# Making the gated layer's node tables inside the attention layer's loop

## The chip, the cores and the metric

The kernel runs on one core of a Trainium2 chip. The metric is device time in microseconds (us) of one execution. Five engines work side by side and meet only through semaphores: TensorE (PE in the profile; its weight loads are listed apart as PEld), VectorE (DVE), ScalarE (ACT), GpSimd (POOL) and SyncE (SP), which here only issues transfers. Each engine executes its own list of instructions in order: an instruction that waits holds up everything behind it on that engine, and nothing on the others unless they wait for it. Transfers between device memory and on-chip memory are issued by an engine's queue (SPq, ACTq) and run beside the engines.

## The reference

Four graph layers run one after the other on 3125 nodes of 128 numbers, with 50,000 edges that come sorted by destination. After each layer its result is added to the input and every row is normalized (mean taken off, divided by the standard deviation). Cut to what matters:

```python
x = ln(x + L0(x))   # 3 x relu(A_norm @ (x @ W) + b), A_norm: weighted adjacency, normalized
x = ln(x + L1(x))   # attention, 4 heads of 32:
                    #   e = sum(leaky_relu(h_l[dst] + h_r[src]) * att);  softmax over a node's edges
                    #   out[dst] += h_r[src] * alpha
x = ln(x + L2(x))   # gated:  z = concat(x[dst], x[src], edge_attr)
                    #   x + segment_sum(sigmoid(z @ W_f + b_f) * softplus(z @ W_s + b_s), dst)
x = ln(x + L3(x))   # 10 x gelu(ln(A_norm @ (x @ W) + b)), plus gelu(ln(x @ res_W + res_b))
```

In the gated layer `z @ W` splits in three: a product of the destination's row, one of the source's row, one of the edge's attributes. The first two need to be worked out once per node, not once per edge. They are the layer's two node tables: `to_dst` (row of a node times the first third of both weight matrices, plus the bias, kept as three bf16 parts that add up to the f32 value) and `to_src` (row times the second third, f32).

## The kernel before

Nodes are cut into 25 row tiles of 128 (`NT`), edges into 392 chunks of 128 (`NCH`), and the chunks into 28 stretches of 14 (`NS`, `SC`). A stretch is worked on in four blocks of 4, 4, 3 and 3 chunks. Because the edges are sorted by destination, a stretch touches one window of 128 consecutive nodes, whose first node is looked up at run time; neighbouring windows overlap, and a stretch's partial sums are handed to the next by a shift matrix.

The stages follow one another. **L0** builds the normalized adjacency matrix into device memory (a "bank" of 35 pieces, about 1.15 MB each) while its first convolution runs, then runs convolutions two and three as dense products with that matrix (`Convolutions`, L620-697; a few pieces stay resident on chip as `adj_k`, the others are streamed as `adj`). In the second half of L0 the attention layer's edge data are prepared too (`Attention.prepare`, L1057). **L1**, the attention layer, is `l1_sorted` (L1149-1341). **L2**, the gated layer, is `l2_sorted` (L1344-1568). **L3** (L1571-1637) runs ten dense convolutions with the same bank.

The loops of L1 and L2 are written out as software pipelines: several stretches are in flight, each in another step. The order on each engine is the order in which the program records the instructions. A helper, `InOrder` (L179-192), chains them, so nearly all instructions of the two loops carry line L187 in the profile and are told apart by their tiles.

One iteration `s` of L1's loop (L1303-1340) runs over four blocks `b`:

- `load(s+1)` (b = 0, L1173): SP loads the window's rows (`hl`) and the edges' destinations (`drow`), POOL issues 14 indirect gathers of the sources' rows into `xj` (six buffers).
- `inputs(s, b)` (L1192): PE sums `h_l[dst]` and `h_r[src]` into `zT` (three PSUM buffers): three bf16 products and one f32 product per chunk. ACT and DVE form the leaky relu.
- `logit` (L1210): PE forms the logits `pe`, two blocks behind. `keep_logits` (b = 1) stores them.
- `messages(s-3)` (b = 0, DVE): weights times gathered rows into `msg`. This frees `xj`.
- `add_up(s-3)` (b = 1, PE, L1275): 14 chunks and the shifted sums of the stretch before into `sums`.
- `rows(s-3)` (b = 2) and `finish(s-3)` (b = 3), on DVE and ACT: division, addition of the old row, normalization. The result is the window's new rows, `y`, which SP stores to `after`.

So on PE one iteration is `inputs(s,0)`, `logit`, `inputs(s,1)`, `logit`, `add_up(s-3)`, `inputs(s,2)`, `logit`, `inputs(s,3)`, `logit`. On DVE the end of an iteration is `y` of stretch s-3, and right behind it stand the `messages` of stretch s-2 for the next iteration's `add_up`.

After the loop the whole of `after` is loaded back to `x` (L1341). L2 then begins with a preamble (L1356-1400): it loads and prepares its own edge data (sources, destinations, local indices), writes a copy of `x` to device memory, clears padding rows and loads its weights. Then it makes both tables, a row tile at a time (L1402-1413): PE transposes all tiles of `x`; per tile PE multiplies with the weights (`pp`), DVE adds the bias, ACT and DVE split the sum into three parts (`three_parts`, L1022), SP stores both tables. L2's loop gathers from `to_src` (POOL, `zj`) and cannot start before that table is complete.

Of the kernel before, what the change touches and what calls it, by code (L numbers as in the profile page):

```python
# [10 lines left out]
I32 = mybir.dt.int32  # L11
# [35 lines left out]
def tile_gnn_stack(ctx: ExitStack, tc: tile.TileContext, a: dict, out: bass.AP):  # L47
# [336 lines left out]
    class SortedEdges:  # L384
# [106 lines left out]
        def matrices(self, pool, c0, n):  # L491
# [14 lines left out]
            low = pool.tile([P, CH, P], BF16, name="of_low", bufs=1)[:, :n]  # L506
            ve.tensor_tensor(columns(low), across(self.lows, P // 2), own(self.low, P // 2), op=OP.is_equal)
            heavy = pool.tile([P, 3, CH, P], BF16, name="heavy")[:, :, :n]
# [254 lines left out]
    def l0_sorted(edges, adj, attention):  # L763


        with (
            tc.tile_pool(name="l0", bufs=1) as one,
            tc.tile_pool(name="l0_rows", bufs=3) as rows,
# [18 lines left out]
            with (  # L787
                tc.tile_pool(name="l0_adj", bufs=4) as stream,
                tc.tile_pool(name="l0_hold", bufs=1) as hold,
            ):  # L790
                load_nodes()
                conv.xs[0] = hold.tile([P, NT, D], F32, name="xs0")
                conv.pieces(stream, hold, 6, InOrder(nc.sync))
                attention.prepare(hold, ps, nc.vector)
                for i in (1, 2):
                    conv(conv.xs[i % 2], *layers[i])
                conv.finish()
                conv.end()
# [240 lines left out]


# [108 lines left out]
    def l1_sorted(at):  # L1149
        right, left, before, after, local, logits = at.right, at.left, at.before, at.after, at.local, at.logits  # L1150
        fresh, src_o, dl, att, bias, apart, step = (at.fresh, at.src_o, at.dl, at.att, at.bias, at.apart, at.step)
        with (
# [6 lines left out]
            with (  # L1159
# [7 lines left out]
                pe_, ve, ac, sp = map(InOrder, (nc.tensor, nc.vector, nc.scalar, nc.sync))  # L1167
# [131 lines left out]
                def finish(s):  # L1299
                    sp.dma_start(after[bass.ds(st[s]["first"], P)], normalized(two, st[s], ve))  # L1300
                    st[s] = {"agg": st[s]["agg"]}
# [4 lines left out]
                for s in range(NS + 4):  # L1306
                    for b in range(NK):
                        if b == 0 and s + 1 < NS:
# [32 lines left out]
            nc.sync.dma_start(x, after[:NP].rearrange("(t p) d -> p t d", p=P))  # L1341


    def l2_sorted():  # L1344
# [6 lines left out]
        with (  # L1351
# [4 lines left out]
            to_dst = dram.tile([NP + P, 3, 2 * D], BF16, name="s2_to_dst")  # L1356
            to_src = dram.tile([NP, 2 * D], F32, name="s2_to_src")
            before = dram.tile([NP + P, D], F32, name="s2_before")
            after = dram.tile([NP + P, D], F32, name="s2_after")
            local = dram.tile([NCH * P], BF16, name="s2_local")  # L1360


            src_i = one.tile([P, NCH], I32, name="src_i")
            nc.sync.dma_start(src_i, a["src_c"])
            dst_i = one.tile([P, NCH], I32, name="dst_i")
            nc.sync.dma_start(dst_i, a["dst_c"])
            dl = one.tile([P, NCH], F32, name="dl")
            nc.vector.tensor_tensor(dl.rearrange("p (s c) -> p s c", c=SC),
                                    dst_i.rearrange("p (s c) -> p s c", c=SC),
                                    first_f[:, :NS, None].to_broadcast([P, NS, SC]), op=OP.subtract)  # L1370
            order = one.tile([P, NS, SC], I32, name="order")
            v = a["dst_r"]
            nc.sync.dma_start(order, bass.AP(tensor=v.tensor, offset=v.offset,
                                             ap=[[SC, P], [SE, NS], [1, SC]]))
            lrow = one.tile([P, NS, SC], BF16, name="lrow")
            nc.vector.tensor_tensor(lrow, order, first_f[:, :NS, None].to_broadcast([P, NS, SC]),
                                    op=OP.subtract)
            nc.sync.dma_start(local.rearrange("(s p c) -> p s c", p=P, c=SC), lrow)

            zero = one.tile([P, 3 * D], F32, name="zero")  # L1380
            nc.vector.memset(zero, 0.0)
            zero_b = one.tile([P, 6 * D], BF16, name="zero_b")
            nc.vector.memset(zero_b, 0.0)
            nc.scalar.dma_start(to_dst[NP:].rearrange("p a b -> p (a b)"), zero_b)
            nc.scalar.dma_start(before[NP:], zero[:, :D])
            nc.scalar.dma_start(after[NP - P:NP], zero[:, :D])
            nc.sync.dma_start(before[:NP].rearrange("(t p) d -> p t d", p=P), x)

            w2 = one.tile([D, 3, 2, D], F32, name="w2")
            for s, name in enumerate(("L2_gnn_W_f", "L2_gnn_W_s")):  # L1390
                nc.scalar.dma_start(w2[:, :, s, :], a[name].rearrange("(r k) d -> k r d", k=D))
            b2 = one.tile([P, 2, D], F32, name="b2")
            for s, name in enumerate(("L2_gnn_b_f", "L2_gnn_b_s")):
                v = a[name]
                nc.scalar.dma_start(b2[:, s, :], bass.AP(tensor=v.tensor, offset=v.offset, ap=[[0, P], [1, D]]))
            eps = one.tile([P, 1], F32, name="eps")
            nc.vector.memset(eps, EPS)
            apart = one.tile([P, P], F32, name="apart")
            step = one.tile([P, NS], F32, name="step")
            window_shifts(apart, step, nc.vector)  # L1400

            with tc.tile_pool(name="s2_ps0", bufs=2, space=PSUM) as ps:  # L1402
                xT = transposed_x(one, ps)
                for t in range(NT):
# [296 lines left out]
```

## Time and profile before

| | us |
|---|---|
| time, median of 3 runs (lowest to highest) | 3730.04 (3726.81 to 3734.39) |
| the profiled execution: time / span | 3739.19 / 3736.9 |
| L0: adjacency and first convolution / second and third convolution | 0-361 / 361-672 |
| L1 (attention): start and loop / last `y` | 680-1450 / 1450.1 |
| between L1's last `y` and L2's first gather | 1450.1-1528.5 |
| L2 (gated): loop | 1528.5-2319 |
| L3: ten convolutions | 2319-3737 |

The span is the profiled part of one execution. A line of a timeline gives the start and the duration in us, the engine, the source line, the operation and its tiles as out<-in, how many instructions are merged, and in brackets the idle time before and what ended it ("issue" means that the profile shows nothing that the engine waited for). A line of a group gives count, busy time, the mean of one in ns, and the idle time before such instructions with its releasers. Windows give busy time of each engine, the granted clock of PE as a share of full speed, and the busy share of the DMA engines.

### The profile page before, as it was taken

What the parts mean: (1) busy time and instruction counts of PE and PEld (TensorE: products, weight loads), DVE (VectorE), ACT (ScalarE), POOL (GpSimd) and SP (SyncE); (2) the same over time, 40 slices, a digit from 0 to 9 for tenths busy, and PEclk for the clock granted to TensorE, in tenths of its full rate; (3) what the DMA queues carried; (4) which work ended last, traced back from release to release, by engine and by line L of the source; (5) the groups of instructions that cost most, each with busy time, mean ns of one, the idle gap of its engine ahead of it and who ended that gap; (6) DMA issues with size and microseconds to landing.
All of it is one profiled execution on the core that took longest, in us unless ns stands there. A gap on an engine that the chain in (4) does not pass through costs nothing.

```text
span 3736.9 us, 35807 instructions
## 1 busy us (share of the span) xinstructions
PE 2962.6 (79%) x12881; PEld 1905.5 (51%) x12909; DVE 1632.0 (44%) x4381; ACT 886.0 (24%) x1404; POOL 817.4 (22%) x863
## 2 busy tenths in 40 slices
PE   2898999346667575366666666999999999999998
PEld 2665455235666563155555554555555555555554
DVE  5995112124545455265656656522222222222234
ACT  0332001100111112254544445211111111111112
POOL 3210000544555530445454451000000000000000
PEclk8999999667667677678787888999999999999999
DMA  1345977222323224444444443867667667666665
GB/s 51 131 148 183 337 250 248 76 58 66 74 73 80 66 68 96 148 120 140 121 141 122 132 134 111 283 213 232 217 210 226 213 219 235 208 210 230 220 209 187
DMA packets 420199, 605.98 MB, mean 162 GB/s; under 512 B 76655, under 2 KB 386748, under 8 KB 419996
## 3 DMA queue, kind: packets, MB, share of 16 engines
q1 hardware_dynamic: 373176, 516.45, 43.2%
q0 software_dynamic: 32320, 79.09, 7.6%
q10 hardware_dynamic: 14516, 8.07, 0.7%
q8 instruction: 103, 1.69, 0.2%
q14 instruction: 84, 0.69, 0.1%
HBM read 541.08 MB, written 62.61 MB: 162 GB/s over the span
## 4 chain that ended last, share of the span: by engine, by line
PE 70%; issue 13%; DVE 9%; DMA 3%; POOL 2%; another core or an unknown queue 2%; ACT 1%; SPq 0%; POOLq 0%; DVEq 0%; ACTq 0%
PE acc L674 41%; PE sums L187 7%; PE pz L187 7%; PE zT L187 5%; PE acc L187 3%; PE pe L187 2%; POOL xj L215 2%; PE side L187 2%; PE po L689 2%; DVE heavy L187 2%; DVE z L187 1%; DVE of_low L187 1%; DVE of_pair L187 1%; DMA x<-s_after 1%
## 5 line engine op out<-in xcount | busy, mean ns | idle before, releaser
L674 PE MATMUL acc<-adj_k,xs 128*128 128x460 f32 (+1 forms) x3180 | 1213.1, 537 | 1.3 <-DMA adj_k<-bank 1.3
L674 PEld LDWEIGHTS acc<-adj_k,xs 128*128 128x128 f32 x3180 | 598.9, 190 | 558.2 <-issue 501.3
L215 POOL DMA_INDIRECT xj<-s_right,src_o x392 | 372.0, 949 | 655.2 <-ACT parts L1142 338.5
L215 POOL DMA_INDIRECT zj<-s_to_src,src_i x392 | 370.7, 946 | 527.6 <-DVE z L187 256.8
L187 PE MATMUL sums<-msg,of_edge 128*128 128x132 f32 (+1 forms) x1568 | 290.3, 337 | 210.8 <-issue 194.4
L674 PE MATMUL acc<-adj,xs 128*128 128x460 f32 (+1 forms) x1020 | 404.2, 543 | 2.1 <-DMA adj<-bank 2.1
L187 PEld LDWEIGHTS sums<-msg,of_edge 128*128 128x128 f32 x1568 | 259.9, 244 | 233.1 <-issue 216.6
L187 PE MATMUL pz<-w,eaT 128*128 128x256 f32 x784 | 266.5, 425 | 83.0 <-issue 43.5
L704 DVE SCALAR_TENSOR_TENSOR v<-po,dinv,three 128x128 f32<-128x128 f32 x250 | 71.1, 344 | 576.0 <-PE po L689 574.8
L674 PEld LDWEIGHTS acc<-adj,xs 128*128 128x128 f32 x1020 | 192.8, 191 | 186.3 <-issue 174.4
L187 DVE TENSOR_TENSOR z<-pz,zj 128x1024 f32<-128x1024 f32 (+1 forms) x112 | 121.9, 1088 | 309.4 <-remote 241.2
L187 PE MATMUL zT<-ident,xj 128*128 128x128 f32 x784 | 156.7, 330 | 121.5 <-issue 111.0
L187 PEld LDWEIGHTS zT<-ident,xj 128*128 128x128 f32 x784 | 140.5, 238 | 155.8 <-issue 139.5
L187 PE MATMUL pz<-td,of_node 128*128 128x256 bf16 x1176 | 208.2, 289 | 13.7 <-DVE of_node L187 8.4
L187 ACT ACTIVATE leaky<-zT 128x512 f32<-128x512 f32 (+1 forms) x112 | 60.3, 541 | 625.2 <-PE zT L187 362.4
L187 DVE TENSOR_TENSOR leaky<-zT,leaky 128x512 f32<-128x512 f32 (+1 forms) x112 | 68.9, 616 | 316.6 <-ACT leaky L187 193.2
L716 ACT ACTIVATE rs<-rs 128x4 f32<-128x4 f32 (+1 forms) x91 | 18.6, 205 | 786.0 <-DVE rs L715 786.0
L187 ACT ACTIVATE soft<-z 128x1024 f32<-128x1024 f32 (+1 forms) x112 | 106.4, 950 | 388.2 <-DVE z L187 245.5
L187 PE MATMUL pe<-att,leaky 128*128 128x4 f32 x784 | 117.0, 262 | 102.1 <-issue 95.8
L187 PEld LDWEIGHTS pz<-w,eaT 128*128 128x128 f32 x784 | 133.0, 213 | 105.9 <-issue 52.6
L187 PEld LDWEIGHTS pe<-att,leaky 128*128 128x128 f32 x784 | 125.1, 231 | 102.1 <-issue 94.4
L187 PEld LDWEIGHTS <-of_node 128*128 128x128 bf16 x1176 | 123.0, 105 | 90.5 <-issue 21.7
(195 smaller groups left out, 3309.8 us busy)
## 6 DMA issues: line engine op xcount, KB each, us to landing
adj_k<-bank SPq DMA_DIRECT2D x268, 1150.0 KB
adj_k<-bank SPq DMA_DIRECT2D x50, 912.5 KB
bank<-strip SPq DMA_DIRECT2D x6, 5750.0 KB
adj<-bank SPq DMA_DIRECT2D x14, 1150.0 KB
eaT<-in_ea_t SPq DMA_DIRECT2D x56, 256.0 KB
drow<-s_local SPq DMA_DIRECT2D x28, 448.0 KB
eaT<-in_ea_t SPq DMA_DIRECT2D x56, 192.0 KB
drow<-s_local SPq DMA_DIRECT2D x56, 128.0 KB
```

The source lines that it names most:

```text
L187: ins = getattr(self.engine, name)(*args, **kwargs)
L215: after_writers(nc.gpsimd.indirect_dma_start(out=to, out_offset=None, in_=table[:NP, :], in_offset=bass.IndirectOffsetOnAxis(ap=index[:, c ...
L674: lanes.tensor.matmul(acc[:, :c1 - c0], xs[:, t, :], k[:, q, :c1 - c0], start=(t == 0), stop=(t == NT - 1))
L689: lanes.tensor.matmul(po[:, t - t0, :], self.aggT[:, t * P:(t + 1) * P], w, start=True, stop=True)
L704: lanes.vector.scalar_tensor_tensor(to[:, t - t0, :], sums[:, t - t0, :], dinv[:, t:t + 1], bias, op0=OP.mult, op1=OP.add)
L716: nc.scalar.activation(rs[:, :n], rs[:, :n], AF.Sqrt)
```

## The change

The two tables are made in L1's loop, from `y` of each stretch, while it is on chip. `next_rows(s, stage)` does it in five stages, each placed at the head of a block: at b = 0 of the iteration after `y` PE transposes `y` and ACT copies the result (stage 0), at b = 1 PE multiplies with the weights, ACT evicts the source half and SP stores it (1), then DVE adds the bias and ACT makes the first part (2), and DVE and ACT make the second (3) and third (4), which SP stores at the head of the next iteration. The transpose and the product use the loop's `zT` buffers. The loop is one iteration longer. There are 28 windows in place of 25 tiles; rows in two windows are written twice.

A class `Gated` loads and prepares the layer's edge data and weights in the second half of L0, beside those of the attention layer. L2's preamble, the copy of `x`, the reload of `x` behind L1 and the table loop are gone: L2 reads L1's `after` as its old rows, and one set of in-order chains serves L1 and L2.

The longer-lived tiles take room from others: 5 adjacency pieces stay resident in L0 in place of 6, and 8 in L3 in place of 9; `l0_rows` has two buffers in place of three; the one-buffer tile `of_low` becomes a part of `heavy`, whose third part is made in place.

```diff
-            low = pool.tile([P, CH, P], BF16, name="of_low", bufs=1)[:, :n]
+            heavy = pool.tile([P, 3, CH, P], BF16, name="heavy")[:, :, :n]
+            low = heavy[:, 2]
...
-            tc.tile_pool(name="l0_rows", bufs=3) as rows,
+            tc.tile_pool(name="l0_rows", bufs=2) as rows,
...
-                conv.pieces(stream, hold, 6, InOrder(nc.sync))
+                conv.pieces(stream, hold, 5, InOrder(nc.sync))
                 attention.prepare(hold, ps, nc.vector)
+                gated.prepare(hold, nc.vector, attention.dl)
...
+        def prepare(self, scratch, ve, dl):
...
+            zero = scratch.tile([P, 2 * D], F32, name="zero_g")
+            ve.memset(zero, 0.0)
+            nc.sync.dma_start(self.to_src[NP - P:NP], zero)
+            nc.sync.dma_start(self.after[NP - P:NP], zero[:, :D])
+            nc.sync.dma_start(self.src_i, a["src_c"])
+            dst_i = scratch.tile([P, NCH], I32, name="dst_g")
+            nc.sync.dma_start(dst_i, a["dst_c"])
+            ve.tensor_tensor(self.dl.rearrange("p (s c) -> p s c", c=SC), dst_i.rearrange("p (s c) -> p s c", c=SC),
+                             first_f[:, :NS, None].to_broadcast([P, NS, SC]), op=OP.subtract)
+            lrow = scratch.tile([P, NCH], BF16, name="lrow_g")
+            ve.tensor_copy(lrow, dl)
+            nc.sync.dma_start(self.local.rearrange("(s p c) -> p s c", p=P, c=SC),
+                              lrow.rearrange("p (s c) -> p s c", c=SC))
...
                 def finish(s):
-                    sp.dma_start(after[bass.ds(st[s]["first"], P)], normalized(two, st[s], ve))
-                    st[s] = {"agg": st[s]["agg"]}
+                    t = st[s]
+                    y = normalized(two, t, ve)
+                    sp.dma_start(after[bass.ds(t["first"], P)], y)
+                    st[s] = {"agg": t["agg"], "first": t["first"], "y": y}
+
+                def next_rows(s, stage):
+
+                    t = st[s]
+                    if stage == 0:
+                        yT = ps_z.tile([D, 4 * P], F32, name="zT")[:, :P]
+                        pe_.transpose(yT, t.pop("y"), ident)
+                        t["yT"] = two.tile([D, P], F32, name="yT", bufs=1)
+                        ac.activation(t["yT"], yT, AF.Copy)
+                    if stage == 1:
+                        t["pp"] = pp = ps_z.tile([P, 4 * P], F32, name="zT")
+                        pe_.matmul(pp, t.pop("yT"), gated.w2[:, :2].rearrange("k r s d -> k (r s d)"),
+                                   start=True, stop=True)
+                        t["parts"] = two.tile([P, 3, 2 * D], BF16, name="parts", bufs=1)
+                        t["row"] = two.tile([P, 2, 2 * D], F32, name="row", bufs=1)
+                        ac.activation(t["row"][:, 1], pp[:, 2 * D:], AF.Copy)
+                        sp.dma_start(gated.to_src[bass.ds(t["first"], P)], t["row"][:, 1])
+                    if stage == 2:
+                        ve.tensor_add(t["row"][:, 0], t.pop("pp")[:, :2 * D],
+                                      gated.b2.rearrange("p s d -> p (s d)"))
+                    if stage > 2:
+                        ve.tensor_sub(t["row"][:, 0], t["row"][:, 0], t["parts"][:, stage - 3])
+                    if stage > 1:
+                        ac.activation(t["parts"][:, stage - 2], t["row"][:, 0], AF.Copy)
+                    if stage == 4:
+                        sp.dma_start(gated.to_dst[bass.ds(t["first"], P)], t["parts"])
+                        st[s] = {"agg": t["agg"]}
...
-                for s in range(NS + 4):
+                for s in range(NS + 5):
                     for b in range(NK):
+                        for r, stage in ((s - 5, b + 4), (s - 4, b)):
+                            if 0 <= r < NS and stage < 5:
+                                next_rows(r, stage)
...
-            nc.sync.dma_start(x, after[:NP].rearrange("(t p) d -> p t d", p=P))
...
-            nc.sync.dma_start(before[:NP].rearrange("(t p) d -> p t d", p=P), x)
...
-                xT = transposed_x(one, ps)
-                for t in range(NT):
-                    pp = ps.tile([P, 2, 2, D], F32, name="pp")
-                    nc.tensor.matmul(pp, xT[:, t * P:(t + 1) * P], w2[:, :2], start=True, stop=True)
-                    h = two.tile([P, 2, 2, D], F32, name="h")
-                    nc.vector.tensor_add(h[:, 0], pp[:, 0], b2)
-                    nc.scalar.activation(h[:, 1], pp[:, 1], AF.Copy)
-                    parts = two.tile([P, 3, 2, D], BF16, name="parts")
-                    evict = three_parts(parts, h[:, 0])
-                    nc.sync.dma_start(to_src[t * P:(t + 1) * P, :].rearrange("p (s d) -> p s d", d=D), h[:, 1])
-                    nc.sync.dma_start(to_dst[t * P:(t + 1) * P].rearrange("p i (s d) -> p i s d", d=D), parts)
...
-            conv.pieces(stream, one, 9)
+            conv.pieces(stream, one, 8)
```

## The prediction

> **What bounds the kernel now.** I read the slices of the page first, then windows for each stage, then the timelines of the two places that the change touches. The windows:
>
> ```profile
> core 0: us, PE busy (x) PEld busy (x) DVE busy (x) ACT busy (x) POOL busy (x), PEclk, DMA share, GB/s
> 820.00:1400.00 580.00, 382.36 (x2296) 342.74 (x2318) 294.29 (x988) 62.78 (x165) 292.45 (x308) 0.71 0.29 72
> 1450.00:1530.00 80.00, 38.49 (x75) 13.54 (x75) 35.75 (x89) 37.78 (x101) 1.23 (x2) 0.71 0.63 161
> 2352.00:3736.00 1384.00, 1368.12 (x4010) 721.59 (x4008) 433.81 (x1565) 272.98 (x348) 0.00 (x0) 1.00 0.67 219
> ```
>
> L3 is PE's: 1368 of 1384 us busy at the full clock. L1's steady loop (820-1400) fills no engine: PE 66% at a granted clock of 0.71, DVE 51%, POOL 50%, ACT 11%. Its period is 25 us a stretch (`add_up` starts on PE at 998.8, 1024.0, 1048.8, 1073.8). A loop with no full engine is bound by a chain that goes round between them. The table stage (1450-1530) has nothing beside it but itself. Its edges:
>
> ```profile
> 1450.11 0.34 DVE L187 TENSOR_SCALAR y<-u,mv,rs 128x128 f32<-128x128 f32 x1
> 1451.52 2.43 SPq L187 DMA_DIRECT2D s_after<-y  x1
> 1457.24 0.80 SPq L1341 DMA_DIRECT2D x<-s_after  x1
> 1465.84 3.84 PE L603 MATMUL xT_ps<-ident,x 128*128 128x128 f32 x16 [19.48 <-DMA x<-s_after]
> 1528.46 0.95 POOL L215 DMA_INDIRECT zj<-s_to_src,src_i  x1 [159.31 <-ACT parts L1025]
> ```
>
> From the last `y` to L2's first gather: 1528.46 - 1450.11 = 78.4 us, of it 15.7 for a store and a reload, the rest for 25 transposes and tiles.
>
> The loop, where the change puts this work, on PE in one stretch, and DVE's `y` (three answers of the timeline):
>
> ```profile
> 1006.17 0.38 PE L187 MATMUL zT<-of_node,hl 128*128 128x512 bf16 x1
> 1007.84 0.38 PE L187 MATMUL zT<-of_node,hl 128*128 128x512 bf16 x1 [1.29 <-issue]
> ...
> 1017.04 0.37 PE L187 MATMUL zT<-ident,xj 128*128 128x128 f32 x1 [1.75 <-issue]
> 1018.45 0.57 PE L187 MATMUL zT<-ident,xj 128*128 128x128 f32 x1 [1.04 <-issue]
> 1018.81 1.28 PE L187 MATMUL pe<-att,leaky 128*128 128x4 f32 x6
> 1019.95 1.44 PE L187 MATMUL zT<-of_node,hl 128*128 128x512 bf16 x3
> 1021.19 1.91 PE L187 MATMUL zT<-ident,xj 128*128 128x128 f32 x8
> 1022.89 1.28 PE L187 MATMUL pe<-att,leaky 128*128 128x4 f32 x6
> 1024.03 1.23 PE L187 MATMUL sums<-msg,of_edge 128*128 128x132 f32 x4
> ```
> ```profile
> 1014.16 0.35 DVE L187 TENSOR_SCALAR y<-u,mv,rs 128x128 f32<-128x128 f32 x1
> ```
> ```profile
> 1022.86 0.94 POOL L215 DMA_INDIRECT xj<-s_right,src_o  x1 [7.15 <-PE zT L187]
> ```
>
> PE starts `inputs(s,0)` at 1006.17, 8.3 us before the `y` of the stretch four back is there (1014.51). It then crawls, an instruction in 1.4 to 2.1 us for no reason but "issue", until shortly after POOL's run of 14 gathers (998.5-1015.7). Then it goes densely but at half speed: the second block takes 3.1 us here, 1.7 in a dense stretch at 872.3. `add_up` follows at 1024.0. POOL has been idle 7 us by then, so gathers are not what is late.
>
> **The change part by part** (against the profiled execution, 3739.2 us, which lies 9.2 above the median).
>
> *D, the gap between L1 and L2, goes.* Left after the last `y`: transpose (0.5), eviction (0.35), product (the pair of passes 1.0 to 1.9), eviction (0.4), a store. The pair store-reload above needed 5.7 us from issue to the follower's issue. That is 0.5+0.35+1.6+0.4+5 = about 8. Gain 78.4 - 8 = **-71**. `to_dst` follows some 2 us behind `to_src`; its reader, PE's `pz`, first ran 9 us after the first gather, so that is covered.
>
> *B, the loop.* Per stretch PE gets one transpose (rows of L603: 272 to 475 ns) and one product of 128x512 (L1406, two passes of 592 to 1222 ns, mean 787), ACT five evictions of about 0.4, DVE three of 0.42, SP two stores. By busy time alone that is 2 us of PE. The place matters more: the transpose is PE's first instruction of the iteration and waits for `y`. Behind it stand `inputs(s,0)`, `logit`, the product, `inputs(s,1)`, `logit` and `add_up`, so all that PE did ahead of `y` now comes after it. I took each steady and draining stretch (23 of them, the `y` of stretches 1 to 23), and put after `y` the whole sequence, once at the dense rows (transpose 0.27 + 1.70 + 0.73 + product 1.02 + 1.70 + 0.73 = 6.15 us) and once at half-speed rows (0.47 + 3.15 + 1.28 + 1.90 + 3.15 + 1.28 = 11.2), and compared with where `add_up` starts today. In the stretch shown: 1014.5+6.15 = 1020.7, 3.4 us before 1024.0 (hidden), or 1025.7, 1.7 after it. With `y` at 1194.4 and `add_up` at 1197.2 it is +3.3 or +8.4; with 1087.0 and 1099.3, -6.2 or -1.1. Counting only positive ones, the 23 sum to +32 at dense and +103 at half speed. With every stretch counted, a gain too where PE would be earlier, they sum to -22 and +94. PE will have stood idle for 148/23 = 6.4 us before each `y`, and half-speed rows are what follows such pauses, but it will also have spared instructions for which it crawls now; I take the middle of the positive sums, +68. DVE's and ACT's extra instructions stand in the same round (`y`, `messages`, `rows`): two of the eight, 0.42 each, 0.8 x 23 = +19; none if idle time takes them, which DVE has (286 of 580 us). **B = +87**, bounds -22 and +103+19 = +122; all 148 us of lead lost, and 2 us of new work in each, would be 148+46 = +194.
>
> A rule weighed here. The Trainium skill, "TensorE: Matmul & The Clock Gate", section "HAM oscillation — how this bites in real kernels", says that pauses of PE beyond about 3.4 us put its clock back to half, each time anew. By the rule every one of the 20 stretches whose lead is above 3.4 us would pay half speed, and the sum is near +103. The rows bear it out after the crawl (3.1 against 1.7 us above) but show the clock back before the end of `add_up`, which loses only its first half.
>
> *The drain of L1* (the last four stretches, `y` 11 to 13 us apart): `add_up` starts 0.75 us behind `y` today and then waits for `messages`. Transpose, eviction and product come before it: about 0.5+0.5+1.9 = 2.9, less 0.3 that overlaps: 4 x 2.6 = **+10** (0 to +12).
>
> *A, L0's second half.* SP's queue today has the load of `order`, then the first `adj` (issued 369.29, landed 377.14; PE waits). The new order puts before it two clearing stores, `wide`, `dst_g`, and the store of `lrow_g`, which waits for `dl`, made from `order` (373.07). Such a store of 28-byte runs took 3.62 us to issue (at 1458.15). The first `adj` is issued at about 373.6+3.6 = 377 in place of 369: **+8** (+4 to +12). ACT's `s_local` stores, PE's `side` and the rest of `prepare` are unchanged. The other new loads (`src_i`, weights, biases) stand earlier in SP's list, beside the first convolution, while PE computes: 0.
>
> *C, L1's start.* With no preamble behind it, three of L3's resident pieces (3 x 1150 KB) are now loaded at L1's start, beside the first gathers and `hl`. DMA's share there is 0.19, and the pieces are 11 to 12 us of transfer at the 300 GB/s that the heaviest stretches move (317 from 361 to 400): **+4** (0 to +10).
>
> *E, L3's start.* Today two of those pieces enclose the last store, and the load of `x` behind them is issued 9.1 us after the store (2319.22, 2328.32), against 5.7 in the unloaded case at 1451.52; it takes 10.4 to land against 8.5. Without them **-6** (-9 to -3).
>
> *At nothing:* one piece less resident: L3 loads 27 in place of 26 per layer (DMA share 0.67 to 0.70) and L0's two layers 30 in place of 29 (0.69 to 0.84), under a PE that is full; if that cover went, 1.15 MB at 300 GB/s, 3.8 us a layer. `heavy` in place and `l0_rows` at two: their DVE runs beside a full PE; `of_low` had one buffer anyway, so bounds are -2 and +4. The reload of `x` behind L1 and the ACT table load are in D.
>
> Sum: -71 + 87 + 10 + 8 + 4 - 6 = **+32**. 3739.2 + 32 = 3771; less 9.2 for the median, **3762 us**.
>
> **Rivals.**
> 1. *The loop swallows it (faster).* The crawl ends near the arrival of `y` (1018 against 1014.5 above), and an instruction not issued in it is not lost if PE is fed while it waits. Then PE starts after `y` with a full supply and B is between -22 and +32. For it: six of the 23 stretches come out earlier even at half speed. Against it: 11 come out later even at dense speed. It decides below B = 55, where the sum is zero. With B = +5 the sum is -50: 3680.
> 2. *The wait adds in full (much slower).* If PE's round through `y` becomes the bound, with the pause, half clock and crawl all in it, B goes to +194 or so: sum +139, 3869. For it: `messages` stand right behind `y` and free `xj` for POOL, so a late `y` moves the next gathers and their crawl as well. Against it: in 12 of the 23 stretches `add_up` comes 6 to 14 us after `y` today, so there is room.
> 3. *The gap remains in part.* L2's first gathers wait for something else (the last `to_dst`, `td`, instruction supply: today the first `z` is made at 1555, 27 us behind the first gather), and D is -45: sum +58, 3788. For it: L2's PE crawls during its first gathers today; but those gathers start 70 us sooner either way.
>
> **How the numbers follow.** My forecast (B between +47 and +150) has 0.55, rival 1 0.30, rival 2 0.05, rival 3 0.10. Of the forecast's 0.55 some 0.04 lie within 0.2% (7.5 us, about what a measurement of this kernel can tell from no change), of rival 1's 0.30 some 0.03. So faster 0.27, same 0.07, slower 0.66. The forecast's own range is 3722 to 3825. For 8 in 10 the range reaches down into rival 1 to B = +10 (3685) and up past rival 3 to 3835.
>
> **What would show it.** In the profile after: `y` to L2's first `zj` about 8 us (D; over 25 makes rival 3); on PE a wait of the transpose for `y` at the head of each iteration, around 6 us; spacing of `add_up` about 28 to 29 us where it is 25 (25 or less makes rival 1, over 33 rival 2); DVE's spacing of the last four `y` 14 to 15; the first `adj` issued at 376 or later; L3's load of `x` some 6 us behind the store. The prediction is wrong if PE's crawl shortens by as much as the wait is long, or grows with the longer period.

## The result and the profile after

The changed kernel takes 3793.26 us (median, 3785.81 to 3797.35) beside 3731.53 for the kernel before: ratio 1.0164 (95% interval 1.0144 to 1.0184), 62 us slower. The forecast was 32 us slower. The direction and the range hold the result; the forecast's size is about half of what came.

Chips differ here, and no number below can be understood without this: with unchanged code the kernel before takes 3700 to 3740 us on some chips and 3207 us on others. The first measurement and two later sets of runs met the first kind, four sets the second. On the first kind PE crawls in the two loops: beside POOL's runs of gathers it issues an instruction only now and then, for no reason that the profile shows (the prediction shows such a stretch). I call the two kinds chips with and without the slow stretch. Each kernel is compared only with the kernel before on its own chip.

The stages in the traces, each worked out from start or end times of the named instructions (us):

| | before | after | | before, second chip | after, second chip |
|---|---|---|---|---|---|
| first product of the second convolution | 377.1 | 393.1 | | 376.6 | 392.0 |
| from there to L1's first gather | 303.3 | 302.7 | | 303.3 | 302.8 |
| first gather to `y` of stretch 1 | 191.5 | 190.3 | | 182.7 | 191.7 |
| `y` of stretch 1 to 21 (per stretch) | 491.1 (24.55) | 590.7 (29.53) | | 497.3 (24.87) | 585.6 (29.28) |
| `y` of 21 to 27 | 87.5 | 91.1 | | 81.0 | 91.4 |
| last `y` to L2's first gather | 78.0 | 8.9 | | 78.8 | 8.9 |
| L2's gathers to its last `y` | 790.7 | 790.7 | | 789.6 | 790.7 |
| last `y` to the end | 1417.7 | 1416.0 | | 1418.6 | 1417.2 |
| span | 3736.9 | 3783.6 | | 3727.9 | 3780.2 |

The steady loop's window (same columns as in the prediction):

```profile
850.00:1450.00 600.00, 359.56 (x1993) 304.79 (x2014) 269.39 (x903) 91.24 (x241) 269.00 (x283) 0.70 0.28 72
```

Only ACT is fuller (15% for 11%); PE is at 60% where it was 66%, DVE and POOL at 45% where they were at 51% and 50%. The loop waits more; no engine has become its bound. One stretch of the loop, from `y` to the next `y`, on PE, on DVE and on POOL (timelines of the changed kernel):

```profile
1093.17 0.45 PE L187 MATMUL zT<-ident,y 128*128 128x128 f32 x1 [3.40 <-DVE y L187]
...
1094.69 1.91 PE L187 MATMUL zT<-ident,xj 128*128 128x128 f32 x8
1096.40 1.28 PE L187 MATMUL pe<-att,leaky 128*128 128x4 f32 x6
1097.54 2.05 PE L187 MATMUL zT<-w,yT 128*128 128x512 f32 x2
...
1102.01 0.73 PE L187 MATMUL pe<-att,leaky 128*128 128x4 f32 x6
1102.60 3.40 PE L187 MATMUL sums<-msg,of_edge 128*128 128x132 f32 x28
1105.83 0.39 PE L187 MATMUL sums<-agg,shift 128*128 128x132 f32 x2
...
1111.92 0.17 PE L187 MATMUL pe<-att,leaky 128*128 128x4 f32 x1 [1.03 <-issue]
1112.64 0.56 PE L187 MATMUL pe<-att,leaky 128*128 128x4 f32 x2 [0.56 <-issue]
1114.74 0.48 PE L187 MATMUL zT<-of_node,hl 128*128 128x384 bf16 x1 [1.53 <-issue]
1115.45 0.81 PE L187 MATMUL zT<-of_node,hl 128*128 128x384 bf16 x2 [0.23 <-issue]
1116.87 1.44 PE L187 MATMUL zT<-ident,xj 128*128 128x128 f32 x6 [0.60 <-issue]
```
```profile
1106.23 0.41 DVE L187 TENSOR_TENSOR row<-zT,b 128x256 f32<-128x256 f32 x1
1117.00 0.29 DVE L187 COPY agg<-sums 128x132 f32<-128x132 f32 x1 [10.36 <-PE zT L187]
...
1122.51 0.34 DVE L187 TENSOR_SCALAR y<-u,mv,rs 128x128 f32<-128x128 f32 x1
```
```profile
1096.92 0.95 POOL L215 DMA_INDIRECT xj<-s_right,src_o  x1 [12.62 <-PE zT L187]
```

The transpose waits 3.40 us for `y`, as foreseen. But the costly wait is another: `add_up` ends at 1106.2, and DVE takes its sums only at 1117.00, 10.8 us later, when PE's crawl is over. In the stretch of the kernel before that the prediction shows, the crawl lay in `inputs(s,0)`, beside DVE's work on `y`, and `agg` came 1.9 us after `add_up`'s end:

```profile
1002.01 0.39 PE L187 MATMUL sums<-agg,shift 128*128 128x132 f32 x2
1004.29 0.30 DVE L187 COPY agg<-sums 128x132 f32<-128x132 f32 x1 [1.65 <-PE zT L187]
```

Now it lies between `add_up` and the `agg` that `y` hangs on. What `agg` waits for is PE's signal: in all 20 steady stretches of the changed kernel it starts 0.02 us after a semaphore event of PE, and in 17 of them (13 of 20 on the second chip) that event is one of a bunch of six or more within 1.2 us, though the last product of `add_up` is listed as ended 4.5 to 13.4 us earlier. (The trace lacks some of PE's events, 168 of 2141.) So while PE crawls, the other engines learn late even of products that PE's rows show as done. Averages over 20 stretches, worked out from the traces (the end of `y` to `add_up`'s start; `add_up`; its end to the start of `agg`; from there to the end of the next `y`; and POOL's pause between two runs of gathers):

| | `y`→`add_up` | `add_up` | →`agg` | →`y` | POOL's pause |
|---|---|---|---|---|---|
| before | 7.3 | 5.6 | 2.0 | 9.6 | 8.3 |
| after | 8.3 | 3.6 | 11.1 | 6.6 | 12.5 |
| before, second chip | 8.7 | 5.3 | 1.2 | 9.7 | 7.2 |
| after, second chip | 8.5 | 3.6 | 10.3 | 6.9 | 12.3 |

The gap between the layers is gone as forecast (timeline):

```profile
1567.59 0.35 DVE L187 TENSOR_SCALAR y<-u,mv,rs 128x128 f32<-128x128 f32 x1
...
1571.22 0.33 SPq L187 DMA_DIRECT2D s_to_src<-row  x1
...
1576.85 0.94 POOL L215 DMA_INDIRECT zj<-s_to_src,src_i  x1 [108.71 <-issue]
```

And at the second convolution's start, SP's queue and PE (timelines; the kernel before, then the changed one):

```profile
369.29 2.01 SPq L187 DMA_DIRECT2D adj<-bank  x1
371.41 0.46 SPq L1086 DMA_DIRECT2D wide<-s_dst_pad  x1
```
```profile
372.96 0.39 SPq L1122 DMA_DIRECT2D wide<-s_dst_pad  x1
374.06 3.30 SPq L1063 DMA_DIRECT2D dst_g<-in_dst_c  x1
377.45 0.38 SPq L1068 DMA_DIRECT2D s_local<-lrow_g  x1
377.88 3.06 SPq L187 DMA_DIRECT2D adj<-bank  x1
```
```profile
393.10 3.40 PE L674 MATMUL acc<-adj,xs 128*128 128x460 f32 x4 [17.11 <-issue]
```

The first piece is issued 8.6 us later than before (377.88, 369.29), now behind `wide`, and needs 15.2 us to PE's first product in place of 7.9 (377.14 before). From 369 to 393 the DMA engines are full (share 1.09) and move 179 GB/s.

### The profile page after: what moved, and what is told of

It is laid out like the page before. It is cut to its first block, busy times and chain, and to the rows that moved or that the text cites. A ratio compares the mean times of both kernels' runs of the same rounds, so it can differ in the third digit from the quotient of the medians.

```text
span 3783.6 us, 36101 instructions
## 1 busy us (share of the span) xinstructions
PE 2960.8 (78%) x12890; PEld 1904.0 (50%) x12918; DVE 1627.9 (43%) x4379; ACT 900.1 (24%) x1443; POOL 819.1 (22%) x863
## 4 chain that ended last, share of the span: by engine, by line
PE 47%; issue 6%; DVE 3%; another core or an unknown queue 1%; DMA 1%; SPq 1%; ACT 0%; DVEq 0%
PE acc L674 34%; PE pz L187 7%; PE sums L187 4%; PE po L689 1%; DVE z L187 1%; SPq L642 1%; DVE pz L187 0%; DVE gate L187 0%; DVE msg L187 0%; DMA adj<-bank 0%; DVE of_edge L187 0%; DMA adj_k<-bank 0%; DMA s_after<-y 0%; ACT soft L187 0%
## 5 line engine op out<-in xcount | busy, mean ns | idle before, releaser
L674 PE MATMUL acc<-adj_k,xs 128*128 128x460 f32 (+1 forms) x3300 | 1260.7, 537 | 1.6 <-DMA adj_k<-bank 1.6
L674 PEld LDWEIGHTS acc<-adj_k,xs 128*128 128x128 f32 x3300 | 620.9, 190 | 578.1 <-issue 520.3
L187 PE MATMUL sums<-msg,of_edge 128*128 128x132 f32 (+1 forms) x1568 | 254.9, 308 | 185.3 <-issue 181.3
L674 PE MATMUL acc<-adj,xs 128*128 128x460 f32 (+1 forms) x900 | 356.9, 544 | 17.8 <-issue 17.1
L187 PEld LDWEIGHTS sums<-msg,of_edge 128*128 128x128 f32 x1568 | 227.1, 217 | 206.5 <-issue 201.1
L674 PEld LDWEIGHTS acc<-adj,xs 128*128 128x128 f32 x900 | 171.0, 191 | 183.2 <-issue 169.9
L187 PE MATMUL pe<-att,leaky 128*128 128x4 f32 x784 | 131.0, 268 | 120.9 <-issue 120.1
L187 PEld LDWEIGHTS zT<-ident,xj 128*128 128x128 f32 x784 | 152.2, 261 | 102.7 <-issue 86.2
L187 PEld LDWEIGHTS pe<-att,leaky 128*128 128x128 f32 x784 | 140.7, 249 | 117.2 <-issue 114.6
L187 PEld LDWEIGHTS <-heavy 128*128 128x128 bf16 x1875 | 122.1, 101 | 83.0 <-issue 58.2
```

Source lines behind the costliest of these rows:

```text
L187: ins = getattr(self.engine, name)(*args, **kwargs)
L674: lanes.tensor.matmul(acc[:, :c1 - c0], xs[:, t, :], k[:, q, :c1 - c0], start=(t == 0), stop=(t == NT - 1))
```

## The experiments

**Does the order in L0 cost what the trace shows?** `e1_prepare_later` records the edge data's preparation behind the second convolution:

```diff
-                gated.prepare(hold, nc.vector, attention.dl)
                 for i in (1, 2):
                     conv(conv.xs[i % 2], *layers[i])
+                    if i == 1:
+                        gated.prepare(hold, nc.vector, attention.dl)
```

> The changed kernel with one edit: the gated layer's edge data are prepared behind the second convolution's loads in the order of recording, not ahead of them. Theory: the first adjacency load issues at about 369 us again and the first dense product starts 14 to 16 us earlier than the 393.1 of the changed kernel; the whole time falls by the same 14 to 16 us, to some 3778 us, all later stages unchanged in length. Rival: the late stores only move the same queue time to a later place of the second convolution, where they delay a streamed piece; then the gain is under 6 us.

Measured, on a chip without the slow stretch: 3145.77 us beside 3207.32, ratio 0.9807 (0.9791 to 0.9824). PE's first product is at 364.8; the unchanged order gives 378.9 on such a chip (`e9_after`), 14.1 later. On the second chip with the slow stretch the same edit, in `e5_both`, gives 378.4 against 392.0. So the order costs what the trace shows at the second convolution's start. Of the whole time less came off: 3145.77 us beside the 3156.92 of `e9_after`, 11.2 in place of the 14 to 16 expected and of the rival's 6 at most; 1.9 us of the start is lost again before L1's first gather (303.4 us from the first product, 301.6 in `e9_after`).

**Is it the place of the new stages, or their work?** `e2_behind_add_up` keeps every instruction and moves the stages behind `add_up`, where `y` is always there, since the `messages` that `add_up` needs stand behind it on DVE:

```diff
-                        for r, stage in ((s - 5, b + 4), (s - 4, b)):
-                            if 0 <= r < NS and stage < 5:
-                                next_rows(r, stage)
+                        if b == 3 and 0 <= s - 4 < NS:
+                            next_rows(s - 4, 2)
...
-                    if stage > 1:
+                    if stage > 2:
                         ac.activation(t["parts"][:, stage - 2], t["row"][:, 0], AF.Copy)
...
                             positive(s, b)
+                        if b < 2 and 0 <= s - 5 < NS:
+                            next_rows(s - 5, b + 3)
+                        if b in (1, 2) and 0 <= s - 4 < NS:
+                            next_rows(s - 4, b - 1)
+                        if b == 3 and 0 <= s - 4 < NS:
+                            ac.activation(st[s - 4]["parts"][:, 0], st[s - 4]["row"][:, 0], AF.Copy)
```

> The changed kernel with the five stages moved within the iteration: the transpose behind add_up, the product behind the third block's logits, DVE's and ACT's parts after the normalization, the messages and the placing. All instructions are the same in number. Theory of the wait: PE starts the next stretch ahead of y again; the spacing of add_up falls from 29.7 us to 25 to 27 and the time by 65 to 110 us, to 3685-3730. Rival, theory of the work: the added PE, ACT, DVE and queue instructions are what costs 4.7 us a stretch; the spacing stays at 29 to 30 and the time within 15 us of 3793.

`e3_ready_tile` leaves all in place and transposes a tile that is always ready:

```diff
-                        pe_.transpose(yT, t.pop("y"), ident)
+                        pe_.transpose(yT, ident, ident)
```

> The changed kernel, every instruction where it is, but the transpose reads the identity in place of y, so the tables that it leaves are wrong; PE has no wait for y at the head of the iteration. Theory of the wait: spacing of add_up 25 to 27 us, time 3690-3735, and agg follows add_up by 0 to 3 us in place of 10. Rival, theory of the work: spacing 29 to 30, time within 15 us of 3793.

`e4_half_gathers` leaves the wait and halves POOL's run:

```diff
-                    for c in range(SC):
+                    for c in range(0, SC, 2):
                         gather(t["xj"][:, c, :], right, src_o, s * SC + c)
+                    h = SC // 2
+                    after_writers(sp.dma_start(t["xj"].rearrange("p (c two) d -> p c two d", two=2)[:, :, 1, :],
+                                               right[:h * P].rearrange("(c p) d -> p c d", p=P)), right)
```

> The changed kernel with 7 of the 14 indirect gathers of each stretch in the attention loop replaced by one direct transfer of as many rows (the rows are wrong, the arithmetic the same). Theory of the moved crawl: PE's slow stretch starts 8 to 10 us into a run of gathers and lasts until 2 to 3 us after its end, so a run of 9 us leaves none; agg follows add_up at once and the spacing falls from 29.7 to 19-22 us, the time by 200 to 280 us. Rival: the ring y, inputs, add_up, y is as long without the crawl, since PE only waits for y; spacing 27 to 30, time within 60 us of 3793.

All three met a chip where the kernel before takes 3207 us, and there the question did not arise: 3158.17 us (0.9848), 3153.76 (0.9835) and 3134.20 (0.9770), all with a spacing of 17.5 to 17.7 us. Three more runs of each of the last two met no chip with the slow stretch either. The transpose of the ready tile:

> The same kernel as e3_ready_tile (the transpose reads the identity, the tables are wrong), on whatever chip it meets; on the chip where the kernel before took 3207 us the loop was bound by the gathers and the wait could not show. Where the kernel before takes about 3731: theory of the wait, spacing of add_up 25 to 26.5 us, the time 3700 to 3730, near e5_both plus 14; theory of the work, spacing 29 to 30 and 3775 to 3795.

> The transpose reads the identity in place of y (the tables are wrong). Where the kernel before takes about 3731: theory of the wait, spacing of add_up 25 to 26.5 us, 3700 to 3730; theory of the work, spacing 29 to 30, 3775 to 3795. Where it takes about 3207: 3150 to 3158 as twice before.

> The transpose reads the identity in place of y (the tables are wrong), for a chip on which the kernel before takes about 3731. There: theory of the wait, spacing of add_up 25 to 26.5 us, 3700 to 3730; theory of the work, spacing 29 to 30, 3775 to 3795. Where the kernel before takes about 3207: 3150 to 3158 again.

3155.76, 3156.15 and 3151.71 us beside 3207 to 3208. Half the gathers:

> The same kernel as e4_half_gathers (7 of 14 gathers a stretch in the attention loop replaced by one direct transfer, rows wrong). Where the kernel before takes about 3731, theory of the moved crawl: no slow stretch on PE in a run of 9 us, agg behind add_up at once, spacing 18 to 21 us in place of 29.3, time lower by 170 to 250 us, 3540 to 3615. Rival, the ring through y is as long without it: spacing 27 to 30, time within 60 us of 3785.

> Seven of a stretch's 14 gathers replaced by one direct transfer (rows wrong). Where the kernel before takes about 3731: theory of the moved crawl, agg behind add_up at once, spacing 18 to 21 us, 3540 to 3615; rival, the ring through y alone, spacing 27 to 30, within 60 us of 3785. Where it takes about 3207: 3125 to 3140 as twice before.

> Seven of a stretch's 14 gathers replaced by one direct transfer (rows wrong), for a chip on which the kernel before takes about 3731. There: theory of the moved crawl, agg behind add_up at once, spacing 18 to 21 us, 3540 to 3615; rival, the ring through y alone, spacing 27 to 30, within 60 us of 3785. Where it takes about 3207: 3125 to 3140 again.

3131.22, 3130.87 and 3122.99 us beside the same. What half the gathers would do on a chip with the slow stretch has not been seen, so the test of the crawl that they were meant for is not made.

**Does the sign hang on the slow stretch?** The changed kernel itself, twice, on chips of both kinds:

> The changed kernel itself, beside the kernel before on the same chip. On the chip of the first four experiments the kernel before took 3207 us where it had taken 3731, so the question is whether the sign hangs on that. Theory of the moved crawl (the loss in the loop is PE's slow stretch moved behind add_up): where the kernel before takes about 3207 us, there is no slow stretch, both loops are bound by POOL's gathers at 17.5 us a stretch, the loop costs nothing more, and the change gains the gap of 69 us less 15 at the second convolution: 3150 to 3165, ratio 0.983 to 0.987. Where the kernel before takes about 3731, 3785 to 3800 again. Rival, the wait for y costs 4.7 us a stretch by itself: slower than before by 30 us or more on any chip.

> The changed kernel once more, on whatever chip it meets. Where the kernel before takes about 3207: theory of the moved crawl, both loops bound by POOL at 17.5 us a stretch, 3155 to 3170, ratio 0.984 to 0.988; rival (the wait for y costs 4.7 us a stretch by itself), 3230 or more. Where it takes about 3731: 3785 to 3795 as in both runs so far.

On the second chip with the slow stretch: 3785.47 us beside 3735.27, ratio 1.0145 (1.0125 to 1.0164). On a chip without: 3156.92 beside 3206.93, ratio **0.9846** (0.983 to 0.9863). So the same change loses 50 us on the one and gains 50 on the other. On the latter PE's wait for `y` is there too (waits of 790 to 1110 us: line, total, count, longest), but `agg` is not held up:

```profile
PE zT L187 <- DVE y L187: 47.5, 18, 3.6
```
```profile
790.00:1110.00 320.00, 271.01 (x1815) 232.69 (x1815) 241.92 (x810) 82.24 (x216) 242.40 (x255) 0.86 0.49 123
```

Here the way from `add_up`'s end to `agg` is 0.4 us on average, where the chips with the slow stretch have 10 to 11. POOL is busy 242 us with 255 gathers at a spacing of 1.25 us, 319 of 320: POOL never pauses in this loop (17.87 us a stretch). The ring of the table's columns is 7.9 + 3.6 + 0.4 + 6.0 = 17.9 us, just as long. Half the gathers show that the ring alone would hold the loop there: POOL then pauses about 9 us a stretch, and the spacing stays at 17.6 (`e11_half_gathers`). The kernel before has no profile on such a chip, so what its loop took there is not known.

`p_before` gave the profile of the kernel before on the second chip; it is in the tables.

> The kernel before, for its profile on this chip. Where its time is near 3207: spacing of add_up and of the gated loop's stretches 17.4 to 18 us, POOL without pauses, agg within 2 us of add_up's end. Where it is near 3731: spacings 25 and 27.3 as in the first profile.

The waits of DVE for `agg` in the same window (900 to 1350) of the kernel before and of the changed one on that chip:

```profile
DVE agg L187 <- PE zT L187: 38.9, 13, 5.4
DVE agg L187 <- PE sums L187: 7.3, 3, 2.7
DVE agg L187 <- PE pe L187: 2.4, 1, 2.4
DVE agg L187 <- issue: 2.1, 1, 2.1
```
```profile
DVE agg L187 <- remote: 100.9, 11, 10.5
DVE agg L187 <- PE zT L187: 36.4, 3, 12.9
DVE agg L187 <- PE pe L187: 9.9, 1, 9.9
```

And PE's own wait for `y` in the changed kernel, same window:

```profile
PE zT L187 <- DVE y L187: 58.2, 15, 8.5
```

("remote" stands where a semaphore event ended the wait and the profile finds no instruction that ended just then: the late signals of above.) 51 us of 450 have become 147, in 15 stretches in place of 18: 2.8 and 9.6 a stretch. The wait for `y` is 3.9 a stretch.

**The two edits together**, `e5_both`, on the second chip with the slow stretch:

> The stages moved behind add_up and the edge data prepared behind the second convolution's loads, both edits together. Where the kernel before takes about 3207: no gain in the loop, which the gathers bound, 14 to 16 us from the second convolution: 3138 to 3150. Where it takes about 3731, theory of the wait: 3670 to 3715; theory of the work: 3770 to 3785.

3696.36 us beside 3735.27, ratio 0.9898 (0.9875 to 0.992): 39 us faster than before, 89 faster than the changed kernel, with every instruction of it. Spacing 26.13 where the changed kernel has 29.28 and the kernel before 24.87. The 3.15 us of the difference are thus the place of the stages (of PE's and of DVE's and ACT's together, which the edit moves at once), 1.26 remain. The crawl has moved once more, into `add_up` and behind `agg` (`y`→`add_up` 4.2, `agg`→`y` 14.6), and PE no longer waits for `y`. The gain for the second chip is 20 x 3.15 = 63 us in the steady loop and 13.6 at the second convolution; of the rest of the 89 some 9 lie in the loop's start and drain, 1 is lost again between the layers (10.1 for 8.9), and about 5 are in no row of the two traces, which differ by 83.7.

**The wait alone, on a chip with the slow stretch.** `e16_ready_tile` is `e3_ready_tile` again, on such a chip:

> The transpose reads the identity in place of y (the tables are wrong). Where the kernel before takes about 3731: theory of the wait, spacing of add_up 25 to 26.5 us, 3700 to 3730; theory of the work, spacing 29 to 30, 3775 to 3795. Where it takes about 3207: 3150 to 3158 again.

3720.19 us beside 3710.56, ratio 1.001 (0.9989 to 1.0031), spacing 26.78; the kernel before, profiled on that chip, has 24.31 (`e15_before`). DVE's waits for `agg` in 900 to 1350:

```profile
DVE agg L187 <- remote: 72.7, 8, 10.1
DVE agg L187 <- issue: 9.3, 1, 9.3
DVE agg L187 <- PE zT L187: 8.3, 3, 3.4
DVE agg L187 <- PE pe L187: 2.3, 1, 2.3
```

93 us in place of 147: with the wait for `y` away the hold-up of `agg` shrinks from 9.6 to 5.5 a stretch. The changed kernel was not run beside it; by its spacing in its two profiles with the slow stretch (29.3 to 29.5) an estimate is that about 2.6 of 5 us a stretch are the wait, and the rest is work and order, which no run takes apart. Neither theory is met: the spacing lies just above the 25 to 26.5 of the wait alone. The time is inside its 3700 to 3730, but that range was written for a kernel before of 3731, and here that takes 3710.56: the kernel ends level with it (1.001), where the wait alone had promised 1 to 31 us less.

The kernel before on that chip says something else: it has about the spacing of the other two profiles, but from `y` to `add_up` it takes 11.0 us, and from `agg` to the next `y` 6.8, where the first profile has 7.3 and 9.6. So where the crawl falls in the kernel before differs from one profile to the next.

> The kernel before, for its profile. Where its time is near 3207: attention and gated loop both at 17.4 to 17.6 us a stretch, so that the changed kernel's 17.87 there costs 6 to 12 us over the loop, and the first dense product of the second convolution at 363 to 365 us, 14 to 16 ahead of the changed kernel's 378.9. Where it is near 3731: as in its two profiles.

**A pause in POOL's run.** `e8_paced` is `e5_both` with the second seven gathers of a stretch held until PE's third block:

> e5_both, with the second 7 of a stretch's 14 gathers made to wait on PE's third block of the iteration before, so that POOL pauses after 7 gathers; the work is the same. Where the kernel before takes about 3731, theory that PE slows only 8 to 10 us into an unbroken run of gathers: the slow stretch goes or shrinks to 2 or 3 us, spacing 20 to 24 us in place of 26.1, time 3580 to 3670. Rival, PE slows in proportion to the gathers whatever their spacing: spacing 25 to 28, time 3680 to 3750. Where the kernel before takes about 3207: 0 to 40 us slower than e5_both, since POOL, the bound there, is made to wait.

> Both edits of e5_both and a pause after 7 of 14 gathers. Where the kernel before takes about 3731: theory that PE slows only 8 to 10 us into an unbroken run, spacing 20 to 24 us, 3580 to 3670; rival, in proportion to the gathers, spacing 25 to 28, 3680 to 3750. Where it takes about 3207: 3165 to 3185 as before.

Twice on chips without the slow stretch (`e8`, `e12`): 3175.18 and 3174.07 us, 0.99 of the kernel before. `e5_both` was not run there; the kernels with one of its two edits took 3145.77 and 3158.17, so the pause costs there. On a chip with the slow stretch it was not run, so whether a pause shortens the crawl stays open.

## Why the prediction was right and wrong

Two terms were mis-sized, A (+8, measured +16) and E (-6, measured -1.7), and of B the path was wrong: the loss in the loop is not the longer way from `y` to `add_up` but PE's late signal from `add_up` to `agg`.

**D, the gap: right.** 78.0 became 8.9 in the trace (by the ends of `y`), -69.1 against -71.

**A, L0's second half: the term that was mis-sized most.** "The first `adj` is issued at about 377 in place of 369: +8". The issue came at 377.88, as worked out. The mistake was to stop at the issue: the piece then took 15.2 us in place of 7.9, with `wide` (1344 KB), `dst_g` and the small-run store now ahead of it and the DMA engines full. +16.0 and +15.4 in the two pairs, twice the term; with the order of `e1` and `e5` 14 of it goes. Which of the transfers ahead costs how much, no run tells.

**E, L3's start: too large.** -6 was forecast; the whole of L3 became 1.7 us shorter in one pair and 1.4 in the other. The store-to-load pair took 7.4 us (2367.65 to 2375.00) and not the 5.7 of the row used, and the load 9.8 to DVE's first use of it where 10.4 were needed before; so `x` is there 2.4 us earlier, and L3 kept 1.4 to 1.7 of that.

**B, the drain and C: the sum right, the path wrong.** Forecast 87 + 10 + 4 = +101 from the first gather to the last `y`; measured 770.1 to 872.1, +102, and +107.7 on the second chip. But I had it as a longer way from `y` to `add_up`, +3 a stretch at the middle of dense and half speed, plus 0.8 for DVE and ACT. That way grew by 1.0 us only, on the second chip not at all (8.7, 8.5), and `add_up` behind it became 2 us shorter. What came is +9 at `agg` on both chips and -3.0 and -2.7 behind it. That my number fits is luck.

What moved the crawl there can be followed in the traces. In the changed kernel a run of gathers begins 3.9 us after the end of `y`, in all 20 stretches on both chips, and 0.65 after the last of the `messages`, which free `xj` and stand right behind `y`. The run lasts 17.4 us; PE's crawl begins about 8 to 11 us into it in nearly all stretches, and the bunch of signals comes 2.8 us after its end. `agg` starts with it in most stretches, and from there to the end of `y` it is 6.6 us: 3.9 + 17.4 + 2.8 + 6.6 = 30.7, where the spacing is 29.5. So the crawl keeps its distance from `y`, and PE's work, pushed behind `y`, changed its place towards it. In the kernel before the distance is not fixed (3.6 to 13.7 us from `y` to the run, 6.9 on average). The profile before showed the links: in rival 2 I named this chain ("a late `y` moves the next gathers and their crawl as well") and did not follow it to what PE would be doing then; I had set POOL aside ("gathers are not what is late"), and the chain runs through its gathers. That this ring sets the period is read from the traces; the run that would have cut it, half the gathers on a chip with the slow stretch, is missing. The crawl itself did not grow: PE's pauses over 0.3 us without a shown reason add up to 153 us in 20 stretches before and 129 after, while its waits for `y` come to 85.

**The rule on the clock.** The Trainium skill ("TensorE: Matmul & The Clock Gate", section "HAM oscillation — how this bites in real kernels") has PE fall back to half speed after pauses of some 3.4 us. The row with the 3.40 us wait does not show that: the granted clock there was at half from 1077.7 to 1101.6, so already in the crawl, 12 us before this wait began. The six logits at 1096.40 took 1.28 us, those at 1102.01 0.73. On the chip without the slow stretch, where PE does not crawl, the waits for `y` of 2.5 to 3.6 us were enough: the granted clock falls to half in each of the 20 iterations, in 15 of them for 3.4 us (`e9_after`, timeline; the same eight products at half and at full clock):

```profile
811.98 0.45 PE L187 MATMUL zT<-ident,y 128*128 128x128 f32 x1 [2.57 <-DVE y L187]
813.50 1.87 PE L187 MATMUL zT<-ident,xj 128*128 128x128 f32 x8
817.39 1.05 PE L187 MATMUL zT<-ident,xj 128*128 128x128 f32 x8
```

So in this loop shorter pauses than the page's 3.4 us count. It is no large part of the loss, though: `y`→`add_up` came out at 8.3 us, between the 6.15 and 11.2 of the two ends, and the clock of the window is 0.70 against 0.71.

**C and the remainder.** Three pieces loaded beside the first gathers: -1.2 in one pair, +9.0 in the other, from gather to `y` of stretch 1; with two such numbers the term can't be told. The drain, +10 in the forecast, was +3.6 and +10.4. L2, the lost resident pieces, `heavy` in place: -0.6 to +1.1 us, put down at nothing.

**The sum.** In profiles +46.7 and +52.3 against +32: A is 8 of the difference, E 4, the rest D and the loop. The medians say +62 and +50. The profiled run of before lay 8 us above its median and that of after 7 below its own, so 15 us of the first pair's 62 are in no row of the two traces, and their cause stays open.

**The rivals.** Rival 1 (the loop swallows it) fits the chips without the slow stretch, where the change gains 50 us, and its thought that PE loses little by waiting through its crawl was right on the others, as far as `y`→`add_up` goes. Rival 2 had the chain that came, at twice the price (+139). Rival 3 (the gap remains) is out.

## What to carry to other kernels

Work put at the head of an in-order engine's iteration does not only wait for its input: all that the engine did ahead of that input moves behind it, and meets whatever else keeps time by the same event. Ask for each such engine what was running beside the work that moves, and where it will stand then. New stages belong behind an instruction that already waits for something later than their input: here behind `add_up`, which with the later preparation turned 1.0145 into 0.9898, with the same instructions. And a transfer that is moved back is priced to its landing, with what is now ahead of it in the DMA engines, not to its issue.

## What the runs showed of the hardware that I had not expected

The same kernel takes 3207 us on some chips and 3700 to 3740 on others. The dense stages are alike (L3 1416 to 1419 us on both); the difference is in the loops with indirect gathers. With the slow stretch L2's loop takes 26.8 to 27.3 us a stretch in every profile, without it 17.5 (of the changed kernel and its variants; the kernel before was not profiled there); in L1 the changed kernel takes 29.3 to 29.5 and 17.9. POOL issues its gathers at the same 1.25 us on both. What differs is PE: between `y` of stretch 1 and 21 of the changed kernel it stands still for over 0.3 us with "issue" as the only reason 151 times (129 us) on the one and never on the other, where all of its 22 pauses wait for `y` or for gathered rows. Instructions of DVE and ACT that need its results start when that ends, on PE's late signals. What makes it is not settled: no run on a chip with the slow stretch changed the gathers themselves, and whether it is the chip or something that passes is not known (the one chip that was met twice was without it both times).
